# A graph layer's edge messages: three instead of four of a chunk's sixteen node tiles taken by one-hot products, and a whole-array product for the node maxima

## The chip, the cores and the metric

The kernel runs on one core of one Trainium2 chip. The metric is the device time of one execution in microseconds (us); lower is better. A core has five engines with a queue of instructions each: PE (TensorE, matmuls; its weight loads are listed as PEld), DVE (VectorE), ACT (ScalarE), POOL (GpSimd) and SP (SyncE, which here only issues DMAs). They run at the same time and wait for each other by semaphores.

## What is computed

For 400,000 edges (sorted by their target node `dst`) between 12,500 nodes of 32 features:

```
h = relu(layernorm(x))                              # 12500 x 32
e = concat(h[src], h[dst], edge_attr)               # 400000 x 96
v = relu(e @ W1 + b1) @ W2 + b2                     # 96 -> 64 -> 32
out = x + maximum(segment_max(v, dst), h)
```

The costly part is `h[src]`: 400,000 rows of 128 bytes at random places.

## The kernel before

**Tiling.** The edges are cut into 4 stripes of 100,000 (`NS`), and the stripes into 196 chunks (`NCH`) of 512 edges (`C`). A chunk therefore holds 4 x 512 = 2048 edges. Its source rows come as 16 tiles (`K`) of 128 rows: in a tile, partitions 32s to 32s+31 hold 32 edges of stripe s.

**Two ways to a source row.** Of the 16 tiles of every chunk but the last, 12 are gathered and 4 (`MM`) are computed:

- `gather(c)` (L150) has POOL issue one indirect DMA for each gathered tile (L156). Its 128 rows of `h_d` in HBM land in a third of a buffer `gh` that holds `SOME = 3` tiles. There are 24 such buffers; a chunk uses four. POOL issues the gathers of all chunks one after another and stops only where no buffer is free.
- `tile(c, m)` (L229) selects 128 rows of `h` by matmuls. `h` stands in on-chip memory as `hs`, in seven groups of 14 nodes a partition and in two parts whose sum has the full precision. For each of 7 groups and 2 parts a matmul multiplies a one-hot `hot` (128 places x 128 edges) with `hs` (128 places x 448), 14 in all, into a PSUM tile `pv`. DVE multiplies that with a mask (L244) and reduces it (L245) to the 32 features, `gm`. The one-hots of a chunk are made by DVE (`one_hots`, L209, five groups) and ACT (`one_hots_act`, L218 and L219, two groups); their width is `MM` x 128.

`to_features(c, part)` (L247) brings both to a layout with features on partitions: for `part` 0 to 3 DVE transposes one gathered buffer of `SOME` tiles into `ht` (L258), which sets that buffer free for POOL, and for `part = J = 4` it transposes `gm` (L261).

**Main loop** (L535). One turn takes a pair of chunks, and the order of PE, DVE, ACT and SP is written out by hand. With c the pair whose messages are finished and a = c + 2, b = c + 3 the pair whose source rows are being made, PE's order in a turn is: tile(a, 0); the first layer's products with `ht` (L502, `into_ph`); tile(a, 1); tile(a, 2); the first layer's products with the next edge features `ea` (L502); the second layer (L573); the products with the target rows `of` (L502); `leave_2` of chunk c - 1 (L488); tile(a, 3); transposes of chunk c (L478); tile(b, 0); `leave_2` of chunk c; tile(b, 1); transposes of chunk c + 1; tile(b, 2); tile(b, 3). ACT turns the first layer into `hid` (L557); DVE adds a penalty at segment ends and takes a running maximum along the edges in a scan (L580, `sm`), and adds the bias after the transposes (L480, `so`). After each `tile` DVE does that tile's L244 and L245 and the transposes of one gathered buffer.

**PSUM.** `pv` has three buffers. In turn they take each tile's product, the two outputs of the second layer, the transposes and the result of `leave_2`. So a PE step waits for DVE or ACT to have read what stood there three steps before.

**leave_2** (L483) places the maxima of a chunk: for each stripe a window of 32 nodes (`W`), to which `last` holds a one-hot of the last edges. The products are two halves: stripes 0 and 1 into PSUM partitions 0 to 63, stripes 2 and 3 into 64 to 127, four steps of 128 edges each. ACT copies the result to `wo` (L492; three buffers), and SP stores four 32 x 32 blocks to `top_d` (L496), one for each stripe.

Of the kernel before, what the change touches and what calls it, by code (L numbers as in the profile page):

```python
# [8 lines left out]
F32 = mybir.dt.float32  # L9
# [14 lines left out]
P = 128  # L24
N = 12500
E = 400000
D = 32
# [3 lines left out]
NS = 4  # L31
W = 32
C = 512
J = C // P
# [7 lines left out]
LOAD = 4  # L42
A1 = 7
A0 = NT // A1
MM = 4
MMC = range(NCH - 1)
SOME = 3
AHEAD = 4
BLOCK = 14
NB = NCH // BLOCK  # L50
# [12 lines left out]
def ap(t, offset, dims):  # L63
    return bass.AP(tensor=t.tensor, offset=t.offset + offset, ap=dims)
# [3 lines left out]
def gnn_kernel(ctx, tc, x, src, src_mm, src_t, dst, dst_ext, lo, lo_c, ends_b, edge_attr, weights, w1, w2, b2, out):  # L68
# [19 lines left out]
    nc = tc.nc  # L88
# [7 lines left out]
    top_d = [dram.tile([NP, D], F32, name=f"top_d{k}") for k in range(2)]  # L96
    key_d = dram.tile([len(MMC) * MM * P], F16, name="key_d")
    acc_d = dram.tile([NP, D], F32, name="acc_d")
# [31 lines left out]
    hs = const.tile([P, 2, A1, D, A0], F32R, name="hs")  # L130
    place_k = const.tile([P, len(MMC) * MM], F32, name="place_k")

# [17 lines left out]
    def gather(c):  # L150
        n = min(K - MM * (c in MMC), (SE - c * C) // D)
        parts = []
        for k in range(0, n, SOME):
            parts.append(gathered.tile([P, SOME, D], F32, name="gh"))
            for i in range(min(SOME, n - k)):
                nc.gpsimd.indirect_dma_start(  # L156
                    out=parts[-1][:, i, :], out_offset=None, in_=h_d[:, :],
                    in_offset=bass.IndirectOffsetOnAxis(ap=src_i[:, c, k + i:k + i + 1], axis=0))
        return parts
# [3 lines left out]
    early_ps = ctx.enter_context(tc.tile_pool(name="early_ps", bufs=1, space=PSUM))  # L163
# [12 lines left out]
    def group(out, of, last=None):  # L176

        nc.vector.tensor_scalar(out, of, 1.0 / A0, 0.5 / A0 - 0.5, op0=ALU.mult, op1=ALU.add)
        nc.vector.tensor_scalar(out, out, ROUND, None, op0=ALU.add)
        nc.vector.tensor_scalar(out if last is None else last, out, ROUND, None, op0=ALU.subtract)  # L180

    def places(start, stop):

        se = src_i[:, MMC.start + start:MMC.start + stop, K - MM:]
        pk = place_k.rearrange("p (c m) -> p c m", m=MM)[:, start:stop]
        group(pk, se)
        nc.vector.scalar_tensor_tensor(pk, pk, -float(A0), se, op0=ALU.mult, op1=ALU.add)

    def load_keys(c, queue=nc.scalar):

        if c in MMC and c % KEYS == 0:
            n = min(KEYS, MMC.stop - c)
            kb = early.tile([P, KEYS, MM * P], F16, name="kb", bufs=2)
            queue.dma_start(kb[:, :n], ap(key_d, (c - MMC.start) * MM * P,
# [17 lines left out]
    def one_hots_act(c, groups=BY_ACT):  # L212

        if c not in MMC:
            return
        for k in groups:
            away = early.tile([P, MM * P], F32, name="away", bufs=2)
            nc.scalar.activation(away, keys[c], AF.Square, bias=key_n[:, k:k + 1])  # L218
            nc.scalar.activation(hot_of(c)[:, k], away, AF.Relu, bias=ones, scale=-1.0)  # L219

    def mask_of(c):
        if c in MMC:
            masks[c] = early.tile([P, MM, A0], F32, name="mask", bufs=2)
            nc.vector.tensor_tensor(
                masks[c], place_ps[:, None, :].to_broadcast([P, MM, A0]),
                place_k[:, (c - MMC.start) * MM:(c - MMC.start + 1) * MM, None].to_broadcast([P, MM, A0]),
                op=ALU.is_equal)

    def tile(c, m):  # L229

        if c not in MMC:
            return
        if m == 0:
            mm_rows[c] = early.tile([P, MM, D], F32, name="gm", bufs=4)
        hot = hots[c]
        e = slice(m * P, (m + 1) * P)
        po = early_ps.tile([P, C], F32, name="pv", bufs=3)[:, :D * A0]
        for k in range(A1):
            for part in range(2):
                nc.tensor.matmul(po, hot[:, k, e], hs[:, part, k].rearrange("p f a -> p (f a)"),  # L240
                                 start=(k == 0 and part == 0), stop=(k == A1 - 1 and part == 1))
        of_group = po.rearrange("p (f a) -> p f a", a=A0)
        one = early.tile([P, D, A0], F32, name="one", bufs=2)
        nc.vector.tensor_tensor(one, of_group, masks[c][:, m, None, :].to_broadcast([P, D, A0]), op=ALU.mult)  # L244
        nc.vector.tensor_reduce(mm_rows[c][:, m, :], one, axis=AX.X, op=ALU.max)  # L245

    def to_features(c, part):  # L247

        if c >= NCH:
            return  # L250
        if c not in hts:
            hts[c] = early.tile([P, K, D], F32, name="ht", bufs=4)
        ht = hts[c]
        n = min(K - MM * (c in MMC), (SE - c * C) // D)
        if part < J:
            r = slice(part * SOME, min((part + 1) * SOME, n))
            if r.start < n:
                nc.vector.transpose(ht[:, r].rearrange("p k e -> p (k e)"),  # L258
                                    gh[c][part][:, :r.stop - r.start].rearrange("p k f -> p (k f)"))
        elif c in MMC:  # L260
            nc.vector.transpose(ht[:, n:].rearrange("p k e -> p (k e)"),  # L261
                                mm_rows.pop(c).rearrange("p k f -> p (k f)"))
        elif n < K:
            nc.vector.memset(ht[:, n:], 0.0)
# [26 lines left out]
    with tc.tile_pool(name="nodes", bufs=1) as pool, tc.tile_pool(name="nodes_ps", bufs=2, space=PSUM) as ps:  # L291
# [127 lines left out]
        one_hots_act(1, range(3, A1))  # L419
        one_hots(1, 0, 3)  # L420
        mask_of(1)
        for m in range(1, MM):
            tile(0, m)
            to_features(0, m)
        to_features(0, J)
# [3 lines left out]
    with tc.tile_pool(name="edges", bufs=3) as pool, tc.tile_pool(name="edges_ps", bufs=1, space=PSUM) as ps:  # L429
# [52 lines left out]

        def leave_2(c, so, last):  # L483

            pw = early_ps.tile([P, C], F32, name="pv", bufs=3)[:, :2 * D]
            for j in range(J):
                for g in range(2):
                    nc.tensor.matmul(pw[g * 2 * W:(g + 1) * 2 * W],  # L488
                                     last[:, j, 2 * g:2 * g + 2].rearrange("p s w -> p (s w)"),
                                     so[:, j, g * 2 * D:(g + 1) * 2 * D], start=(j == 0), stop=(j == J - 1))  # L490
            wo = pool.tile([P, 2 * D], F32, name="wo")
            nc.scalar.activation(wo, pw, AF.Copy)  # L492
            _, base = windows.pop(c)
            for s in range(NS):
                g = slice(s * W, (s + 1) * W)
                nc.sync.dma_start(top_d[s % 2][bass.ds(base[s], W), :], wo[g, s % 2 * D:(s % 2 + 1) * D])  # L496

        def into_ph(ph, pairs, start, stop):
            for x, (w, e) in enumerate(pairs):
# [18 lines left out]
        for c in range(2):  # L518
            window_hots(c)
        one_hots_act(2)  # L520
        for m in range(MM):
            tile(1, m)
            to_features(1, m)
            if m < 2:
                one_hots(2, *((0, 2), (2, BY_ACT.start))[m])
# [9 lines left out]
        for c in range(0, NCH, 2):  # L535
# [32 lines left out]
            last = [lasts(c)]  # L568
            ph = edges_into(a)
            pv = [early_ps.tile([P, C], F32, name="pv", bufs=3) for x in range(2)]  # L570
# [15 lines left out]
            so = leave_1(c, sms[0])  # L586
# [7 lines left out]
            so = leave_1(c + 1, sms[1])  # L594
# [178 lines left out]
```

## Time and profile before

| | us |
|---|---|
| runs (median; lowest, highest) | 4055.93; 4045.58, 4070.74 |
| the profiled execution | 4066.76 |
| its span, first to last instruction | 4065.0 |
| first gather starts, last gather starts | 23.6, 3936.0 |
| DVE busy, ACT busy | 2232.7, 1106.1 |
| mean granted TensorE clock | 0.939 |

The profile is of one execution. In its group rows stand the line of the kernel, the engine, the operation, what it writes and reads, the number of instructions, then busy us and mean ns of one, then the idle time of that engine just before these instructions and what ended most of it ("issue": nothing that the profile shows). A busy share is an average over the span. The waits that concern the gathers, as the profile adds them up for POOL: it sat idle before a gather 542.8 us until a transpose of a gathered buffer (L258), 455.2 us until the transpose of `gm` (L261), and 619.2 us with nothing shown. A timeline row is a start, a duration and what ran; a window row gives the busy time of each engine in a stretch of the span.

### The profile page before, as it was taken

Reading aid. Unit: us, or ns where it says so; the run is one execution under the profiler, and the core shown is the slowest. Engines: PE = TensorE matmul, PEld = TensorE weight load, DVE = VectorE, ACT = ScalarE, POOL = GpSimd, SP = SyncE. Lnnn points to the kernel's source line nnn. Section 1 sums busy time; section 2 is a strip of 40 time slices with the busy share of each in tenths; the row PEclk is TensorE's granted clock in tenths of the full one; section 3 lists DMA queues with packets and bytes.
Section 4 is the critical chain, followed back from the end, with each engine's and each line's share of the span. In section 5 each row is a group of like instructions: output and inputs, shape, how many; then the busy total and the mean of one; then the engine's idle time right before and its main releaser. Section 6 shows DMA issues by size and latency. Waiting matters only on the chain. (4 is left out here: it accounts for less than half of the span.)

```text
span 4065.0 us, 52812 instructions
## 1 busy us (share of the span) xinstructions
PE 3500.2 (86%) x18053; PEld 2584.2 (64%) x18053; DVE 2232.7 (55%) x3876; ACT 1106.1 (27%) x1795; POOL 2257.0 (56%) x2376
## 2 busy tenths in 40 slices
PE   4688889888888898888988888998888889998896
PEld 3466666666666666666666666666666666666665
DVE  4355556555555555555555555555555555655555
ACT  3122222222222222222222232322222223222231
POOL 6555555555555556555555555555555555555550
PEclk7799999999999999999999999999999999999998
DMA  5122212211222122111322222222122222211221
GB/s 189 46 48 65 52 44 55 68 43 44 54 65 49 44 51 69 46 44 46 71 49 47 62 58 47 44 70 52 44 46 66 53 47 49 70 48 44 57 59 50
DMA packets 188622, 229.27 MB, mean 56 GB/s; under 512 B 117549, under 2 KB 159933, under 8 KB 175550
## 3 DMA queue, kind: packets, MB, share of 16 engines
q10 hardware_dynamic: 26692, 110.63, 8.7%
q1 hardware_dynamic: 86618, 76.67, 7.7%
q0 software_dynamic: 75040, 38.57, 6.3%
q8 instruction: 143, 2.34, 0.2%
q14 instruction: 129, 1.06, 0.1%
HBM read 211.76 MB, written 13.85 MB: 56 GB/s over the span
## 5 line engine op out<-in xcount | busy, mean ns | idle before, releaser
L156 POOL DMA_INDIRECT gh<-h_d,src_i x2345 | 2236.5, 954 | 1685.9 <-issue 619.2
L240 PE MATMUL pv<-hs,hot 128*128 128x448 f32 x10920 | 2434.7, 378 | 231.8 <-issue 166.7
L240 PEld LDWEIGHTS pv<-hs,hot 128*128 128x128 f32 x10920 | 2077.6, 194 | 509.9 <-issue 258.1
L244 DVE TENSOR_TENSOR one<-pv,mask 128x448 f32<-128x448 f32 x780 | 478.3, 613 | 1590.8 <-remote 653.4
L557 ACT ACTIVATE hid<-ph,wt 128x512 f32<-128x512 f32 x392 | 254.6, 686 | 1498.2 <-PE ph L502 920.7
L209 DVE TENSOR_TENSOR hot<-kb,consts 128x1536 fp32r<-128x1536 f16 (+2 forms) x388 | 566.1, 1459 | 0.0
L245 DVE TENSOR_REDUCE gm<-one 128x32 f32<-128x448 f32 x780 | 483.6, 620 | 26.9
L219 ACT ACTIVATE hot<-away,ones 128x512 fp32r<-128x512 f32 x392 | 283.6, 724 | 337.3 <-issue 326.3
L580 DVE TENSOR_TENSOR_SCAN sm<-pb,sm,pv 128x512 f32<-128x512 bf16 x195 | 248.2, 1273 | 150.5 <-remote 114.7
L492 ACT ACTIVATE wo<-pv 128x64 f32<-128x64 f32 x196 | 43.8, 223 | 1052.8 <-PE pv L488 765.0
L573 PE MATMUL pv<-hid,wt 128*64 128x512 f32 x784 | 242.1, 667 | 62.2 <-issue 36.3
L488 PEld LDWEIGHTS pv<-so,last 128*64 128x64 f32 x3136 | 126.0, 140 | 250.7 <-issue 162.0
L488 PE MATMUL pv<-so,last 128*64 128x64 f32 x3136 | 166.1, 232 | 131.9 <-issue 121.7
L218 ACT ACTIVATE away<-kb,key_n 128x512 f32<-128x512 f16 x392 | 277.7, 708 | 0.0
L502 PE MATMUL ph<-ea,wt 64*128 64x512 f32 x784 | 233.8, 632 | 35.2 <-issue 29.8
L502 PE MATMUL ph<-ht,wt 64*128 64x512 f32 x784 | 209.7, 637 | 48.3 <-DVE ht L261 42.7
L258 DVE STREAM_TRANSPOSE ht<-gh 128x96 f32<-128x96 f32 x782 | 209.7, 268 | 0.0
L502 PE MATMUL ph<-of,qw 64*128 64x512 f32 x784 | 206.0, 635 | 2.8 <-issue 2.7
L573 PEld LDWEIGHTS pv<-hid,wt 128*64 128x64 f32 x784 | 57.1, 143 | 235.2 <-issue 161.4
L502 PEld LDWEIGHTS ph<-of,qw 64*128 64x128 f32 x784 | 71.9, 195 | 145.4 <-issue 139.3
L502 PEld LDWEIGHTS ph<-ea,wt 64*128 64x128 f32 x784 | 78.3, 188 | 129.5 <-issue 116.2
L502 PEld LDWEIGHTS ph<-ht,wt 64*128 64x128 f32 x784 | 65.2, 188 | 138.2 <-DVE ht L261 77.8
(78 smaller groups left out, 1014.1 us busy)
## 6 DMA issues: line engine op xcount, KB each, us to landing
ea<-in_edge_attr SPq DMA_DIRECT2D x49, 1024.0 KB
db<-in_dst_ext ACTq DMA_DIRECT2D x48, 1024.0 KB
gh<-h_d,src_i POOLq DMA_INDIRECT x2345
pb<-pen_d ACTq DMA_DIRECT2D x48, 512.0 KB
kb<-key_d ACTq DMA_DIRECT2D x47, 512.0 KB
qw<-q_d SPq DMA_DIRECT2D x784, 8.0 KB
top_d<-wo SPq DMA_DIRECT2D x784, 4.0 KB
top_d<-zero ACTq DMA_DIRECT2D x2, 1568.0 KB
```

The costliest lines, as they stand in the source:

```text
L156: nc.gpsimd.indirect_dma_start(out=parts[-1][:, i, :], out_offset=None, in_=h_d[:, :], in_offset=bass.IndirectOffsetOnAxis(ap=src_i[:, c, ...
L209: nc.vector.tensor_tensor(hot_of(c)[:, start:stop], keys[c][:, None, :].to_broadcast([P, n, MM * P]), key_ps[:, start:stop, None].to_broad ...
L218: nc.scalar.activation(away, keys[c], AF.Square, bias=key_n[:, k:k + 1])
L219: nc.scalar.activation(hot_of(c)[:, k], away, AF.Relu, bias=ones, scale=-1.0)
L240: nc.tensor.matmul(po, hot[:, k, e], hs[:, part, k].rearrange("p f a -> p (f a)"), start=(k == 0 and part == 0), stop=(k == A1 - 1 and par ...
L244: nc.vector.tensor_tensor(one, of_group, masks[c][:, m, None, :].to_broadcast([P, D, A0]), op=ALU.mult)
L245: nc.vector.tensor_reduce(mm_rows[c][:, m, :], one, axis=AX.X, op=ALU.max)
L488: nc.tensor.matmul(pw[g * 2 * W:(g + 1) * 2 * W], last[:, j, 2 * g:2 * g + 2].rearrange("p s w -> p (s w)"), so[:, j, g * 2 * D:(g + 1) * ...
L502: nc.tensor.matmul(ph[2 * x + k], w[g], e[g], start=start, stop=stop)
L557: nc.scalar.activation(hid[s], ph[s], AF.Relu, bias=b1c)
L573: nc.tensor.matmul(pv[x][k * 2 * D:(k + 1) * 2 * D], w2x, hid[2 * x + k], start=True, stop=True)
L580: nc.vector.tensor_tensor_scan(sm, loaded.pop(c + x)[2], pv[x], before, op0=ALU.add, op1=ALU.max)
```

## The change

```diff
-MM = 4
+MM = 3
 MMC = range(NCH - 1)
-SOME = 3
+SOME = 4
...
     def tile(c, m):
 
-        if c not in MMC:
+        if c not in MMC or m >= MM:
             return
...
-        for m in range(1, MM):
+        for m in range(1, J):
             tile(0, m)
             to_features(0, m)
...
         def leave_2(c, so, last):
 
-            pw = early_ps.tile([P, C], F32, name="pv", bufs=3)[:, :2 * D]
+            pw = early_ps.tile([P, C], F32, name="pv", bufs=3)[:, :NS * D]
             for j in range(J):
-                for g in range(2):
-                    nc.tensor.matmul(pw[g * 2 * W:(g + 1) * 2 * W],
-                                     last[:, j, 2 * g:2 * g + 2].rearrange("p s w -> p (s w)"),
-                                     so[:, j, g * 2 * D:(g + 1) * 2 * D], start=(j == 0), stop=(j == J - 1))
-            wo = pool.tile([P, 2 * D], F32, name="wo")
+                nc.tensor.matmul(pw, last[:, j].rearrange("p s w -> p (s w)"), so[:, j],
+                                 start=(j == 0), stop=(j == J - 1))
+            wo = pool.tile([P, NS * D], F32, name="wo", bufs=2)
             nc.scalar.activation(wo, pw, AF.Copy)
...
-                nc.sync.dma_start(top_d[s % 2][bass.ds(base[s], W), :], wo[g, s % 2 * D:(s % 2 + 1) * D])
+                nc.sync.dma_start(top_d[s % 2][bass.ds(base[s], W), :], wo[g, s * D:(s + 1) * D])
...
-        for m in range(MM):
+        for m in range(J):
             tile(1, m)
             to_features(1, m)
```

Three of a chunk's sixteen tiles are computed by one-hot products and 13 are gathered. A gather buffer holds four tiles, so a chunk's gathered rows lie in buffers of 4, 4, 4 and 1, each transposed in one instruction. The calls `tile(a, 3)` and `tile(b, 3)` of the loop do nothing; the transposes behind them stay, of the buffer with one tile. `leave_2` multiplies all 128 window rows with all 128 columns of `so` in one matmul for each step of 128 edges, and the four 32 x 32 blocks on the diagonal are what is stored; its two copies `wo` are twice as wide, and there are two instead of three.

## The prediction

> **What bounds the kernel now.** I read the page first, then the waits, then timelines and windows of single stretches.
>
> ```profile
> PE 3500.2 (86%) x18053; PEld 2584.2 (64%) x18053; DVE 2232.7 (55%) x3876; ACT 1106.1 (27%) x1795; POOL 2257.0 (56%) x2376
> ...
> L156 POOL DMA_INDIRECT gh<-h_d,src_i x2345 | 2236.5, 954 | 1685.9 <-issue 619.2
> ```
>
> Taken alone this says that TensorE is the bound. The pairs of chunks say otherwise. Below, columns are the window, its length, then busy time and instructions of PE, PEld, DVE, ACT, POOL, the granted clock, the DMA share and GB/s.
>
> ```profile
> 56.00:137.00 81.00, 17.59 (x36) 9.71 (x36) 7.21 (x22) 5.45 (x8) 61.05 (x64) 0.52 0.35 105
> ...
> 3954.90:3987.60 32.70, 32.70 (x186) 25.17 (x184) 22.29 (x38) 10.88 (x18) 0.44 (x1) 1.00 0.02 5
> 2001.00:2039.00 38.00, 36.54 (x185) 25.99 (x185) 21.97 (x38) 11.20 (x18) 22.91 (x25) 0.96 0.41 96
> ```
>
> The last two rows hold the same work, one pair. After the last gather (3936.0 us) a pair takes 32.7 us with TensorE without a hole; with gathers beside it this one takes 38.0, and the mean from the first scan (172 us) to the one at 3920 is 39.9. The first row is the extreme: POOL issues 64 gathers without a pause, and TensorE gets 36 records done in 81 us, where a matmul of a tile normally follows the last after 0.21 us. So a long unbroken run of gathers holds up the other engines. In the steady part it shows as signals that come late (timeline of DVE, then of POOL; columns: start, duration, what, the idle time before it and what ended that):
>
> ```profile
> 2021.65 0.27 DVE L258 STREAM_TRANSPOSE ht<-gh 128x96 f32<-128x96 f32 x1
> 2021.84 1.18 DVE L209 TENSOR_TENSOR hot<-kb,consts 128x1024 fp32r<-128x1024 f16 x1
> 2032.56 0.62 DVE L244 TENSOR_TENSOR one<-pv,mask 128x448 f32<-128x448 f32 x1 [9.53 <-PE ph L502]
> ```
>
> ```profile
> 2015.46 0.95 POOL L156 DMA_INDIRECT gh<-h_d,src_i  x1 [1.56 <-DVE ht L258]
> 2016.71 0.95 POOL L156 DMA_INDIRECT gh<-h_d,src_i  x1 [0.30 <-issue]
> ...
> 2029.48 0.95 POOL L156 DMA_INDIRECT gh<-h_d,src_i  x1 [0.44 <-issue]
> 2034.29 0.95 POOL L156 DMA_INDIRECT gh<-h_d,src_i  x1 [3.86 <-DVE ht L258]
> ```
>
> The product that DVE waits for ended at 2025.2 in TensorE's records. DVE starts 7.3 us later, 2.1 us after POOL's run ended at 2030.4. POOL stopped because all 24 gather buffers were full, and it goes on once that same DVE step has emptied one. Over the steady part I grouped the gathers into runs (a new run where two starts lie over 1.45 us apart): 125 runs of 6, 33 of 9, 60 of 12, 15 of 15, with mean gaps behind them of 2.6, 2.7, 3.4 and 10.2 us. A product that ends 7 to 11 us into a run is typically seen 5 to 7 us late, about 2 us after the run's end. In runs of 15 TensorE works at full rate until 13 us after the run's start and at 2 to 6% of it from 15 to 21 us. So POOL's time is the sum to count: a gather takes 0.952 + 0.305 us (median duration, plus the idle that always follows), 1.257 us, and the span is 23.6 (first gather) + 2345 x 1.257 = 2947.7 + gaps + 127.8 (from the end of the last, 3936.0 + 1.257, to 4065.0), which leaves 966 for the gaps. The group's row agrees: 1685.9 less 2345 x 0.305 is 971. Per pair that is 9.9 us of gaps beside 24 x 1.257 = 30.2 of gathers.
>
> **The change, part by part.** *Gathers.* 195 chunks gather 13 tiles for 12: 195 more, 2540 x 1.257 = 3192.8, so +245.1 on POOL. Nothing hides it where POOL never pauses but for full buffers.
>
> *Products removed.* Two tiles less per pair, each 14 matmuls in 2.9 us on TensorE and 0.613 + 0.620 us on DVE. One-hots narrow from 1024 and 1536 columns (1.18 and 1.73 us) to 768 and 1152; by their slope 0.90 and 1.32, 1.4 us less DVE per pair. A gathered transpose of 96 or 128 columns takes 0.268 or 0.269 alike: zero. ACT's narrower one-hots, and the product's copy, twice as wide (0.223 us, bounded by the 0.69 of a 512-wide op), lie under ACT's idle 1052.8 before that copy.
>
> *Whole-array product (leave_2).* Sixteen 64-column records now take 0.61 us from group to group; eight of 128 columns are bounded by 0.61 (same columns, half the instructions) and 1.22 (all of the present overlap lost). In the rows four 512-column pairs take 1.92 us, 0.43 per 512; 1024 columns one after another give 0.86. I take 0.9: +0.6 us per pair. The Trainium skill (TensorEngine Tiling (Array Packing), Performance Considerations) says that 64-column operands pack two tiles side by side, so this step should cost up to twice; by it alone the sum would take 1.22, another +0.6 us per pair of TensorE work, and 59 us over 98 pairs if TensorE were the bound.
>
> *Output buffers three to two.* A copy waits for the stores of two chunks ago; they are issued 30 us earlier (stores at 2008.98 to 2017.2, the second copy after at 2046.7) and land in microseconds: nothing. Were that cover gone, ACT would hold up a PSUM buffer and, behind it, the next one-hots.
>
> So a pair has 32.7 - 5.8 + 0.6 = 27.5 us of TensorE work, and needs 26 x 1.257 = 32.7 us of POOL. The last three pairs, without gathers, gain 5.2 each: the tail is 127.8 - 15.6 = 112.2.
>
> *Gaps.* This is the unknown. Between their bounds I sketch one pair, with 0 where DVE has emptied tile 1 of the first chunk. POOL starts at 0.5. DVE does one-hots 1.3, a mask 0.2, tile 2 (1.24 + 0.27): empty at 3.0. Then 0.65 and two scans (2.6): at 6.3 the last scan gives back the PSUM buffer that tile 0 of the second chunk needs, and the 1-gather buffer follows at 6.6. (TensorE waits for these scans: tile 3 stood in front of the transposes L478 and covered 2.9 us of it. Queued behind L478 is that tile 0.) POOL has spent 4 + 4 + 1 = 9 gathers by 11.8. Tile 0 ends at 6.3 + 2.9 = 9.2, 8.7 us into the run, so its signal comes 2 us after the run, at 13.8; empty at 15.4, POOL on at 15.9: a gap of 4.1. Second run: 4, then 4 (17.9), 4 and 1 (22), 4 (24): 17 gathers, 21.4 us, to 37.3. The next tile's product ends at about 27, deep in the run; signal 39.3, empty 40.9, gap 4.1 again. Period 40.9, gaps 8.2. The same sketch for the kernel before gives 38.5 with gaps of 8.3, where 9.9 are measured (ratio 1.19). So the freed TensorE time does not shorten the gaps: they come from the late signals. Low end: if a product signalled in the run comes through (it does where TensorE had just waited, lag 0.04 us), the second run is 21 long and the gaps are 4.2 + 1.6 = 5.8. High end: the 10.2 us behind the runs of 15, say 10.5 per pair. I take 8.7, between the sketch and the sketch times 1.19 (9.8): over 98 pairs 853.
>
> Sum: 23.6 + 3192.8 + 853 + 112.2 = 4182 for the profiled execution's span, +117 on 4065. That execution took 4066.8, 10.8 above the median of 4055.9; less that, 4170.
>
> **The rivals.** *TensorE is the bound after all* (86% busy, late signals only harmless). Then the gathers hide in POOL's 44% of idle time until POOL itself binds: 23.6 + 3192.8 + 112.2 + 2 us of gap per pair (196) = 3525, less 11: 3514. For it: the records; against it: the 36 records in 81 us. The Trainium skill (SBUF — State Buffer, Who interferes with whom) says that DMA never contends with a compute engine, only GpSimd and VectorE share a port; by that the gathers would not slow TensorE and this rival's 3514 would come. The trace disagrees: 38.0 against 32.7 us for equal work. *One long run per pair*: gaps of 5.8, 568 in all, 3897 less 11: 3886. For it: TensorE will wait at the ht products (one tile of cover instead of two), and after such waits signals came through. *Break-even*: gaps of 7.5, 735 in all, cancel the 245; 4053. *Collapse*: two buffers of 4 emptied behind each other make runs beyond 13 us common, each with a gap like 10.2; 11 per pair, 1078 in all: 4396. For it: tiles of 4 instead of 3, so runs are 4/3 as long for as many emptied buffers; against it: the 1-gather buffer breaks them. It decides once the mean run passes some 13 gathers. That the edit isn't what it says is no rival: in the changed program's order a chunk has three 14-matmul tiles and its fourth transposes gathered data alone.
>
> **How the numbers follow.** My forecast, gaps of 8 to 10 per pair (4102 to 4298): 0.48. TensorE bound 0.10, one long run 0.18, break-even 0.12, collapse 0.12. The range leaves out the first rival and most of the collapse: 3885 to 4350; the likeliest case's own is 4100 to 4300. This kernel's runs spread over 0.6%, so 1% is what can be told. Faster 0.28 (first two rivals), same 0.12, slower 0.60.
>
> **What would show it.** Gathers: 2540 of 0.95 us with 0.305 behind each. The group's idle: about 775 + 853. Runs of 8 to 17 in place of 6 to 12, and DVE's product of the first chunk's tile 1 again some 2 us after a run's end. A pair without gathers near 27.5 us, with gathers near 41. PE's share should fall to about 70%. I am wrong if gaps per pair fall under 7, or if a gather's pitch moves.

## The result, and the profile after

The changed kernel takes 4097.9 us (median of 8 runs, 4086.7 to 4119.4) and the kernel before 4057.9 beside it (8 runs, 4036.1 to 4070.7): a ratio of 1.0108, 95% interval 1.0079 to 1.0137. It is slower by some 1%; the forecast was 4170 us, 2.8% above 4056. The profiled execution took 4102.3 us, its span is 4099.9.

The page of the changed kernel, the line of busy times and two groups:

```profile
PE 3283.4 (80%) x13755; PEld 2178.5 (53%) x13755; DVE 1863.2 (45%) x3486; ACT 1037.4 (25%) x1795; POOL 2440.5 (60%) x2571
...
L156 POOL DMA_INDIRECT gh<-h_d,src_i x2540 | 2420.0, 953 | 1555.5 <-DVE ht L258 763.8
...
L487 PE MATMUL pv<-so,last 128*128 128x128 f32 x1568 | 229.3, 291 | 86.8 <-DVE so L480 82.4
```

TensorE has 217 us less of busy time than before and the kernel is longer. POOL has the 2540 gathers at the old 0.953 us. Of its idle time, 763.8 us ended with a transpose by VectorE (L258) that emptied a gather buffer: POOL stands with all buffers full, some two times a pair. Its span adds up as before: 23.3 us to the first gather, 2540 x 1.257 = 3192.8, gaps of 774.0 (summed over the starts of the gathers), and 109.8 behind the last one. That is 7.9 us of gaps a pair, where the kernel before had 9.9.

One turn of the pattern, in windows of the changed kernel (columns as in the prediction: window, length, busy time and instructions of PE, PEld, DVE, ACT, POOL, clock, DMA share, GB/s). It begins with a run of 17 gathers (2021.8), which ends at 2043.1; POOL then stands until 2047.6 and makes a run of 9:

```profile
2021.80:2034.80 13.00, 13.00 (x66) 10.70 (x65) 7.82 (x16) 2.33 (x4) 9.95 (x11) 1.00 0.65 143
2034.80:2043.20 8.40, 4.10 (x12) 1.33 (x10) 0.00 (x0) 5.33 (x9) 6.19 (x7) 0.93 0.38 113
2043.20:2047.60 4.40, 2.91 (x8) 1.34 (x9) 1.74 (x4) 0.00 (x0) 0.00 (x1) 0.50 0.26 95
2047.60:2058.90 11.30, 10.69 (x57) 7.50 (x55) 6.92 (x12) 2.52 (x5) 8.57 (x9) 0.94 0.09 15
```

For 13 us TensorE starts 5 matmuls a us beside the gathers, then 1.4 a us until the run ends, and VectorE starts nothing at all. VectorE's timeline over the same time (start, duration, what, idle time before it and what ended that), and TensorE's:

```profile
2029.41 0.92 DVE L209 TENSOR_TENSOR hot<-kb,consts 128x768 fp32r<-128x768 f16 x1
2045.83 0.63 DVE L244 TENSOR_TENSOR one<-pv,mask 128x448 f32<-128x448 f32 x1 [15.50 <-PE ph L500]
2046.49 0.62 DVE L245 TENSOR_REDUCE gm<-one 128x32 f32<-128x448 f32 x1
2047.03 0.30 DVE L258 STREAM_TRANSPOSE ht<-gh 128x128 f32<-128x128 f32 x1
```

```profile
2029.80 5.88 PE L240 MATMUL pv<-hs,hot 128*128 128x448 f32 x28
2035.61 1.13 PE L500 MATMUL ph<-ea,wt 64*128 64x512 f32 x4
2037.32 0.59 PE L500 MATMUL ph<-ea,wt 64*128 64x512 f32 x1 [0.58 <-issue]
2039.43 0.59 PE L500 MATMUL ph<-ea,wt 64*128 64x512 f32 x1 [1.52 <-issue]
2042.22 1.01 PE L500 MATMUL ph<-ea,wt 64*128 64x512 f32 x1 [2.20 <-issue]
```

TensorE's two tiles are done at 2035.7 at the latest. The product that waits for the first of them starts at 2045.8, 2.7 us after the gathers stop; its transpose at 2047.0 empties the buffer on which POOL goes on at 2047.6. "Issue" on TensorE's lines is time in which it waited for nothing that the profile knows.

Two more windows of the changed kernel: the first lies in its first long run of gathers, the second behind its last gather (what POOL does there is another instruction, L545):

```profile
56.00:137.00 81.00, 22.38 (x32) 9.16 (x32) 7.07 (x23) 5.01 (x8) 61.20 (x66) 0.50 0.32 93
...
4001.00:4028.00 27.00, 27.00 (x142) 20.68 (x140) 18.18 (x34) 10.14 (x18) 9.51 (x1) 1.00 0.10 32
```

At the end, with no gathers, a pair takes 27.5 us from scan to scan and TensorE has no hole. At the start, beside 66 gathers in one run, TensorE gets 32 records done in 81 us.

How late a signal is can be counted over the whole trace, from the end of the last of a tile's 14 matmuls to the start of the product on VectorE that waits for it (L244, waits of over 1 us, from 200 us on). In this run 197 of 233 such products start over 2 us late, with a median of 4.0 us; in the kernel before it is 183 of 351, with a median of 2.0.

### The profile page after: what moved, and what is told of

It is laid out like the page before. It is cut to its first block, busy times and chain, and to the rows that moved or that the text cites. A ratio compares the mean times of both kernels' runs of the same rounds, so it can differ in the third digit from the quotient of the medians.

```text
span 4099.9 us, 44559 instructions
## 1 busy us (share of the span) xinstructions
PE 3283.4 (80%) x13755; PEld 2178.5 (53%) x13755; DVE 1863.2 (45%) x3486; ACT 1037.4 (25%) x1795; POOL 2440.5 (60%) x2571
## 3 DMA queue, kind: packets, MB, share of 16 engines
q0 software_dynamic: 81280, 41.78, 6.5%
## 5 line engine op out<-in xcount | busy, mean ns | idle before, releaser
L156 POOL DMA_INDIRECT gh<-h_d,src_i x2540 | 2420.0, 953 | 1555.5 <-DVE ht L258 763.8
L240 PE MATMUL pv<-hs,hot 128*128 128x448 f32 x8190 | 1821.4, 374 | 174.7 <-issue 155.2
L240 PEld LDWEIGHTS pv<-hs,hot 128*128 128x128 f32 x8190 | 1532.4, 192 | 395.3 <-issue 256.8
L244 DVE TENSOR_TENSOR one<-pv,mask 128x448 f32<-128x448 f32 x585 | 360.6, 616 | 1879.8 <-remote 1300.7
L500 PE MATMUL ph<-ea,wt 64*128 64x512 f32 x784 | 444.3, 795 | 297.0 <-issue 261.2
L209 DVE TENSOR_TENSOR hot<-kb,consts 128x1152 fp32r<-128x1152 f16 (+2 forms) x388 | 436.2, 1124 | 0.0
L487 PE MATMUL pv<-so,last 128*128 128x128 f32 x1568 | 229.3, 291 | 86.8 <-DVE so L480 82.4
L487 PEld LDWEIGHTS pv<-so,last 128*128 128x128 f32 x1568 | 200.7, 197 | 184.3 <-issue 116.1
L219 ACT ACTIVATE hot<-away,ones 128x384 fp32r<-128x384 f32 x392 | 241.3, 616 | 18.5 <-issue 5.7
L218 ACT ACTIVATE away<-kb,key_n 128x384 f32<-128x384 f16 x392 | 235.7, 601 | 0.0
L258 DVE STREAM_TRANSPOSE ht<-gh 128x128 f32<-128x128 f32 (+1 forms) x782 | 205.4, 271 | 0.0
```

The costliest lines, as they stand in the source:

```text
L156: nc.gpsimd.indirect_dma_start(out=parts[-1][:, i, :], out_offset=None, in_=h_d[:, :], in_offset=bass.IndirectOffsetOnAxis(ap=src_i[:, c, ...
L209: nc.vector.tensor_tensor(hot_of(c)[:, start:stop], keys[c][:, None, :].to_broadcast([P, n, MM * P]), key_ps[:, start:stop, None].to_broad ...
L487: nc.tensor.matmul(pw, last[:, j].rearrange("p s w -> p (s w)"), so[:, j], start=(j == 0), stop=(j == J - 1))
L500: nc.tensor.matmul(ph[2 * x + k], w[g], e[g], start=start, stop=stop)
```

## The experiments

Two theories were put on record: G, that POOL's gathers and the gaps that late signals make bound the kernel, and T, that TensorE does. Within G, G1 says that making and moving gathers holds the others up, and G2 that any busy POOL does. In the first two batches below, and in the comparison above, the kernel before took 4036 to 4058 us. In the three later batches the same kernel, from the same source, took 3298 to 3299 us. Ratios are always against the kernel before of the same batch, on the same chip. The only trace of the kernel before is that of the comparison above.

### First batch (before: 4036.1 us)

**The whole-array leave_2 alone**, in the kernel before (four tiles, parts of three gathers):

```diff
-                for g in range(2):
-                    nc.tensor.matmul(pw[g * 2 * W:(g + 1) * 2 * W],
-                                     last[:, j, 2 * g:2 * g + 2].rearrange("p s w -> p (s w)"),
-                                     so[:, j, g * 2 * D:(g + 1) * 2 * D], start=(j == 0), stop=(j == J - 1))
+                nc.tensor.matmul(pw, last[:, j].rearrange("p s w -> p (s w)"), so[:, j],
+                                 start=(j == 0), stop=(j == J - 1))
-            wo = pool.tile([P, 2 * D], F32, name="wo")
+            wo = pool.tile([P, NS * D], F32, name="wo", bufs=2)
```

> The kernel before with the whole-array leave_2 alone (four products a chunk, wo in two buffers; still four tiles a chunk by matmuls). Theory G (POOL's gathers and the gaps that late signals make bound the kernel): 2345 gathers as before, gaps of about 966 us as before, so 4058 us within 1%, because the 0.6 us a pair that TensorE loses or gains is not what the pair waits for. Rival T (TensorE bounds): the whole-array group took 0.81 to 0.99 us against 0.61 us in the traces, two a pair, so +0.4 to +0.8 us a pair, +39 to +74 us, a time of 4097 to 4132 us, and the whole of the change's +1% would be here.

4119.3 us, 1.0216 (1.0178 to 1.0253). G missed. T's range in us holds this time only because the kernel before was 22 us faster in this batch: T wanted 39 to 74 us more than before, and 83 came. The gaps are 1020 us, 54 more than the 966 in the trace of the kernel before, and the two spans (4121.2 and 4065.0) differ by 56: what was added is POOL standing still.

**The tiles alone**: MM = 3 and SOME = 4 with the split leave_2 and three wo buffers.

> The change without its whole-array leave_2: three tiles a chunk by matmuls, thirteen by gathers, the split leave_2 and three wo buffers of before. Theory G: 2540 gathers at 1.257 us and gaps as in the changed kernel (774 us), so 4098 us within 1%: the whole of the slowdown is here. Rival T: 39 to 74 us faster than the changed kernel, 4024 to 4059 us.

4325.5 us, 1.0737 (1.0708 to 1.0765). Both missed, T by more: with less of TensorE's work than the kernel before, it is 7% slower. The gaps are 989 us, 10.1 a pair. So the parts alone cost 2.2% and 7.4%, and together 1.1%: their sizes don't add, and the whole-array product (with its two `wo` buffers), dear alone, takes 215 us of gaps (989 less 774) out of the kernel with three tiles.

**Half of the product matmuls** in the changed kernel:

```diff
-            for part in range(2):
-                nc.tensor.matmul(po, hot[:, k, e], hs[:, part, k].rearrange("p f a -> p (f a)"),
-                                 start=(k == 0 and part == 0), stop=(k == A1 - 1 and part == 1))
+            nc.tensor.matmul(po, hot[:, k, e], hs[:, 0, k].rearrange("p f a -> p (f a)"),
+                             start=(k == 0), stop=(k == A1 - 1))
```

> The changed kernel with half of the tile products: the matmuls with the low part of hs are left out (the output lacks that part), 7 matmuls of 128x392 fewer for each of 6 tiles a pair, some 8.7 us of TensorE's 27.5 us a pair. Theory G: gathers stay at 2540 x 1.257 = 3193 us; the gaps shrink by what the late signals carried of this work, at most from 7.9 to about 4 us a pair, so 3720 to 4100 us; I take 3950 us. Rival T (TensorE bounds): 98 x 8.7 = 853 us less, 3250 us or a little more.

4041.8 us, 1.0021 (0.9992 to 1.0051): by the ratios 0.9% of before, some 35 us, less than the changed kernel, where T wants 853. TensorE's busy time fell from 3283 to 2515 us for it. (The matmuls left out have 448 columns, not 392 as the expectation says.) G's range held; its 3950 was too low, for the gaps shrank only from 774 to 727 us.

**Twelve gathers for thirteen** in the changed kernel:

```diff
-        for k in range(0, n, SOME):
+        for k in range(0, min(n, J * (SOME - 1)), SOME):
...
-                                    gh[c][part][:, :r.stop - r.start].rearrange("p k f -> p (k f)"))
+                                    gh[c][min(part, 2)][:, :r.stop - r.start].rearrange("p k f -> p (k f)"))
```

> The changed kernel with twelve instead of thirteen gathers for each of the first 195 chunks (the thirteenth tile is the transpose of the first row block of the third part once more, so the output is of the wrong nodes there); TensorE, VectorE and ScalarE do what they did. Theory G: 195 x 1.257 = 245 us less of gathers, with gaps between 7 and 11 us a pair as in the other patterns, so 3780 to 4150 us; I take 3853 us, gaps unchanged. Rival T: no change, 4098 us within 1%.

3927.0 us, 0.9735 (0.9713 to 0.9757), by the ratios 3.7%, some 150 us, less than the changed kernel. No other engine's work was taken away, so T is out here. (A chunk now holds three buffers and not four, so the 24 buffers reach two chunks further; what that does was not run alone.) Between the two profiled spans (4099.9 and 3922.6) lie 177 us: of the 245 us of gathers, 35 came back as gaps (809) and 32 as a longer tail (142).

### Second batch (before: 4039.9 us)

**No gathers after the first six chunks**; later chunks transpose those rows again:

```diff
         parts = []
+        if c >= 6:
+            return gh[c - 6]
```

> The changed kernel without the gathers of chunks 6 to 195 (those chunks transpose the rows gathered for chunks 0 to 5 again, so their messages are of the wrong nodes); TensorE, VectorE and ScalarE do what they did. Theory G (POOL's stream and the lateness that it causes in the others): the pairs without gathers at the end of the changed kernel's trace took 27.5 us, so some 150 + 97 x 27.5 + 110 = 2930 us, at most 3100 us where the granted clock falls. Rival T (TensorE bounds): no change, 4098 us within 1%.

2853.2 us, 0.7062 (0.7003 to 0.7121). The 97 pairs take 27.5 us each as forecast; around them are 184 us and not the 260 of the forecast, so its 2930 us was too high. A window of it:

```profile
2000.00:2027.00 27.00, 27.00 (x142) 20.52 (x140) 18.37 (x34) 10.14 (x18) 0.00 (x0) 1.00 0.35 89
```

It is the window 4001 to 4028 of the changed kernel once more, in the middle of the program. The 12.9 us between 27.5 and the 40.4 of a usual pair are due to the gathers. And no signal is late: all 284 products that VectorE waited for start 0.04 us after their last matmul.

**Memsets in the gathers' place**:

```diff
+                if c >= 6:
+                    nc.gpsimd.memset(parts[-1][:, i, :], 0.0)
+                    nc.gpsimd.memset(pause, 0.0)
+                    continue
```

> The changed kernel with each gather of chunks 6 to 195 replaced by two POOL memsets, one of the same 128x32 tile and one of a 128x1024 scratch tile, about 1.2 us together, so that POOL is as long busy and the waits for the buffers are the same, but no descriptors are made and no rows move (the messages of those chunks are of zeros). Theory G1 (what holds the others up is the making and moving of gathers): the others run freely beside POOL, the period goes to POOL's own 26 x 1.2 to 1.3 us and a small wait, 33 to 36 us a pair, 3300 to 3650 us. Rival G2 (any busy POOL holds them up): as the changed kernel, 3950 to 4150 us. Rival T: 4098 us within 1%.

3273.1 us, 0.8102 (0.8034 to 0.8170). Two rows of its groups, and windows:

```profile
L159 POOL MEMSET pause<- 128x1024 f32 x2462 | 2345.8, 953 | 110.5
L158 POOL MEMSET gh<- 128x32 f32 x2462 | 190.5, 125 | 447.1 <-DVE ht L263 443.5 <-issue 3.5
```

```profile
56.00:137.00 81.00, 23.64 (x48) 11.53 (x47) 7.07 (x23) 5.43 (x9) 58.25 (x77) 0.55 0.37 104
2000.00:2032.00 32.00, 30.26 (x140) 22.15 (x140) 17.63 (x32) 10.15 (x18) 30.56 (x54) 0.91 0.11 24
600.00:2600.00 2000.00, 1779.57 (x8198) 1299.12 (x8199) 1124.17 (x2052) 595.70 (x1056) 1912.90 (x3461) 0.90 0.20 50
2700.00:3050.00 350.00, 349.35 (x1781) 264.01 (x1778) 239.04 (x447) 126.66 (x226) 25.64 (x330) 1.00 0.24 62
```

The order on POOL is not that of the source. Of the kernel's engines POOL alone has no order written out by hand, and the long memsets, which wait for no buffer, run ahead of their places: some 33 a pair beside 26 short ones, until the last at 2685.5 us. So this is not POOL at the gathers' pitch, and the 3273 us is a mixture: up to there a pair takes 34.1 us, and behind it 27.5.

It decides between G1 and G2 all the same. At the start, where it still gathers, TensorE starves as ever (48 matmuls in 81 us). From 600 to 2600 us POOL is busy for 96% of the time, against 60% in the changed kernel with its pairs of 40.4 us, and the pair of 34.1 is little more than POOL's own 32.6 us of work. TensorE makes 140 matmuls in 32 us there, and all 266 products that VectorE waited for start 0.04 us after their last matmul. A busy POOL makes no signal late; gathers do: G1. Whether it is the making of a gather or the moving of its rows was not run apart.

**Pauses between gathers**, a memset after every four, or after each:

```diff
             for i in range(min(SOME, n - k)):
                 nc.gpsimd.indirect_dma_start(
...
+            if n - k >= SOME:
+                nc.gpsimd.memset(pause, 0.0)
```

> The changed kernel with a POOL memset of a 128x512 scratch tile, about 0.55 us, after every four gathers: six a pair, 3.3 us of POOL. Theory G with a backlog that a short break drains: the gaps of 7.9 us a pair shrink by more than 3.3 us, 36 to 39 us a pair, 3650 to 3950 us. Theory G with a backlog that needs a wait of some 2 us to drain, so that short breaks are only added to POOL's stream: 40.5 + 1 to 3.3 us a pair, 4150 to 4420 us. Rival T: no change, 4098 us within 1%.

> The changed kernel with a POOL memset of a 128x128 scratch tile, about 0.2 us, after every gather: 26 a pair, 5.2 us of POOL or, if it fits into the 0.3 us between two gathers, nothing. Theory G with a rate limit (what the others get done beside gathers grows with the gathers' spacing): the gaps shrink by more than what is added, 36 to 40 us a pair, 3650 to 4050 us. Theory G with a backlog that only an end of the stream drains: 4150 to 4600 us. Rival T: no change.

4368.6 us, 1.0814 (1.0722 to 1.0905), and 4626.1 us, 1.1451 (1.1336 to 1.1565). Neither tests what it was made for, because here too the memsets ran ahead of their places. From the second kernel, POOL's timeline:

```profile
711.93 0.95 POOL L157 DMA_INDIRECT gh<-h_d,src_i  x1 [0.30 <-issue]
712.88 3.11 POOL L160 MEMSET pause<- 128x128 f32 x12
716.49 0.96 POOL L157 DMA_INDIRECT gh<-h_d,src_i  x1 [0.49 <-issue]
717.45 10.01 POOL L160 MEMSET pause<- 128x128 f32 x38
```

The pauses come in bunches. The last one is at 1001 us in the first kernel and at 1731 us in the second. While they last a pair takes 52.8 and 57.9 us (medians), of which some 20 are pauses. So what a short break inside a run of gathers does stays open.

What is left behind the last pause tells something else. There both kernels issue just what the changed kernel does, and yet the gaps are 9.0 us a pair (1200 to 4200 us, and 1900 to 4400 us), where the changed kernel has 8.0 from 300 to 3900 us. The same instructions settle into different patterns of stops, worth 1 us a pair.

### Third and fourth batch (before: 3297.7 and 3297.6 us)

These were made to find what in leave_2 moves the gaps: its number of products (two column halves, eight products), the wo buffers (three), or its place (leave() ahead of tile(a, 2)).

```diff
+            for g in range(2):
+                r = slice(g * 2 * D, (g + 1) * 2 * D)
+                for j in range(J):
+                    nc.tensor.matmul(pw[:, r], last[:, j].rearrange("p s w -> p (s w)"), so[:, j, r],
+                                     start=(j == 0), stop=(j == J - 1))
-            for j in range(J):
-                nc.tensor.matmul(pw, last[:, j].rearrange("p s w -> p (s w)"), so[:, j],
-                                 start=(j == 0), stop=(j == J - 1))
```

```diff
-            wo = pool.tile([P, NS * D], F32, name="wo", bufs=2)
+            wo = pool.tile([P, NS * D], F32, name="wo")
```

```diff
             mask_of(b)
+            leave()
             tile(a, 2)
...
             windows_into(a, ph)
-            leave()
```

> The changed kernel with leave_2's whole-array product cut into two column halves, eight products of 64 columns a chunk instead of four of 128, one PSUM tile, one copy and two wo buffers as in the change. Theory N (in the stretch of a gather run in which TensorE issues under one matmul a us, the number of its instructions counts, not their length; the split leave_2 has 4 more there before the products whose signals end POOL's two stops): the stops lengthen as in tiles_alone, 4325 us within 2%. Rival W (it is the wo buffers, or the copy of 128 columns, that make tiles_alone slower than the change): 4098 us within 1%. Rival R (it is the rhythm into which the pairs fall, that any small shift moves): anything between 4050 and 4350 us, with other lengths of runs than 9 and 17.

> The changed kernel with three wo buffers instead of two, all else as it is. Theory N: nothing waits for the two buffers, 4098 us within 1%. Rival W (the buffers matter): outside of that, towards tiles_alone's 4325 us if three are worse.

> The changed kernel with the call leave() (leave_2 of the pair before: four matmuls, a copy and four DMAs) moved from behind windows_into to ahead of tile(a, 2). Theory N: four matmuls leave the long stretch of TensorE's order between the second chunk's first tile and the tile before it, so POOL's stop ahead of the second chunk's first part (3.4 us a pair in the changed kernel) falls by about 1.5 us, and the one at the first chunk's second part stays: 3950 us, between 3900 and 4060. Theory R: the rhythm breaks, 4100 to 4350 us. Rival T (TensorE bounds): no change, 4098 us.

> As memsets (each gather of chunks 6 to 195 replaced by a memset of the same tile and one of a scratch tile, so no descriptors and no rows), with a scratch tile of 1275 columns instead of 1024, so that two memsets take about 1.257 us as a gather does. Theory G1 (making and moving of gathers holds up the others; a busy POOL does not): POOL's stream becomes 26 x 1.257 = 32.7 us a pair, its waits shrink from the 4.6 us of memsets to 1 to 3 us, 3350 to 3600 us. Rival G2 (a busy POOL, at its gathers' own pitch, holds up the others): 3950 to 4150 us.

3287.9, 3286.8 and 3281.6 us, ratios 0.9972, 0.9971 and 0.9958, all intervals within 0.9944 to 0.9982. The memsets with the wider scratch tile took 3330.7 us, 1.0104, under the 3350 forecast: a pair mostly takes 33.7 to 33.9 us with POOL busy for 97% of 600 to 2600 us. They ran ahead of their places too, until 3199 us, and made no signal late. None of the numbers on record came. The kernel before itself was 740 us faster, and gathers held up nothing. The first three were run again with the changed kernel itself beside them:

> The changed kernel itself, beside the three that follow. The last four kernels ran on a chip on which the kernel before took 3298 us, and POOL's gathers went on without stops. If the chip is of that kind: POOL's stream bounds, 23.3 + 2540 x 1.257 + 98 x 0.24 + some 50 of tail, 3285 us within 0.5%, 0.996 of before. If it is of the kind on which before takes some 4040 us: 1.011 of before within 0.7%.

> The changed kernel with leave_2's product in two column halves (eight products instead of four). On a chip on which the gathers hold up the others: theory N (the number of TensorE's instructions in the starved stretch) about as tiles_alone, 1.05 to 1.08 of before; rival W (wo buffers, copy) 1.01; rival R (rhythm) anything from 1.0 to 1.08 with other run lengths than 9 and 17. On a chip on which they don't: 0.997 of before.

> The changed kernel with three wo buffers instead of two. On a chip on which the gathers hold up the others: theory N 1.01 of before within 1%; rival W towards 1.07; rival R anything between. On a chip on which they don't: 0.997 of before.

> The changed kernel with leave() moved ahead of tile(a, 2). On a chip on which the gathers hold up the others: theory N 3950 us, 0.965 to 1.0 of before, POOL's stop ahead of the second chunk's first part about 1.5 us shorter than 3.4; rival R 1.01 to 1.08 with the rhythm broken. On a chip on which they don't: 0.996 of before.

The changed kernel took 3281.8 us, 0.9955 (0.9939 to 0.9972), as expected for a chip where gathers hold up nothing; the others 0.9965, 0.9958 and 0.9957, no different from it. A third run of the eight products, in the last batch, gave 0.9968 (0.9958 to 0.9978):

> The changed kernel with leave_2's product in two column halves (eight products instead of four), once more, for a chip on which the gathers hold up the others. There: theory N (the number of TensorE's instructions in the starved stretch) about as tiles_alone, 1.05 to 1.08 of before; rival W (wo buffers, copy) 1.01; rival R (rhythm) anything from 1.0 to 1.08 with other run lengths than 9 and 17. On a chip on which they don't: 0.9965 of before, as twice before.

What these batches do tell is in the page of the changed kernel run again, beside which stand the same lines of the result above:

```profile
PE 2873.5 (88%) x13755; PEld 2120.1 (65%) x13755; DVE 1892.3 (58%) x3486; ACT 1020.0 (31%) x1795; POOL 2441.5 (74%) x2571
...
L156 POOL DMA_INDIRECT gh<-h_d,src_i x2540 | 2421.2, 953 | 803.0 <-issue 572.4
...
L244 DVE TENSOR_TENSOR one<-pv,mask 128x448 f32<-128x448 f32 x585 | 359.6, 615 | 429.4 <-PE pv L240 428.7
```

and in its first 81 us of gathers:

```profile
56.00:137.00 81.00, 63.89 (x288) 44.59 (x286) 38.21 (x71) 25.02 (x43) 61.50 (x65) 0.85 0.42 120
```

It is the same program, with the same gathers at the same 1.257 us, 65 of them in this window as against 66. TensorE made 32 records beside them there and 288 here. POOL's idle time of 803.0 us is little but the 0.305 us behind each gather (2540 x 0.305 = 775); the gaps are 22.7 us in all, and all but 34 of the gathers lie in runs of 45 to 208. All 199 products that VectorE waited for start 0.04 us after their last matmul. The whole is 23.7 + 3192.8 + 22.7 + 39.1 = 3278.3: POOL's stream with nothing in it to shorten but gathers. How many matmuls TensorE starts per us, by the time since a run of gathers began (worked out from the two traces, for runs between 300 and 3900 us; runs split at starts more than 1.45 us apart):

```
us into the run     0-4   4-8   8-12  12-16  16-20  20-30  30-60
in the result      3.57  4.82   4.88   2.80   0.58   0.53      -
run again          4.34  4.62   5.04   5.35   5.48   4.77   3.84
```

The gathers' own rows are no slower where the others are held up. In the run of the result the packets of the gathers' queue (q0) take 6.5% of 16 engines' span, in the run again 9.4%, for the same 81280 packets: 52 and 61 ns each. The last of a gather's packets starts a median of 2.03 us after the gather in the first, and 2.13 us in the second. A rival, that row packets pile up in the DMA engines late in a run, finds no support in these two traces.

### Last batch (before: 3299.3 us)

**A version between the two**: four tiles by matmuls in even chunks, three in odd ones, the split leave_2, gather parts of four in 18 buffers.

```diff
+    def mm(c):
+        return (MM - c % 2) * (c in MMC)
...
-        n = min(K - MM * (c in MMC), (SE - c * C) // D)
+        n = min(K - mm(c), (SE - c * C) // D)
...
-        e = slice(m * P, (m + 1) * P)
+        km = m + MM - mm(c)
+        e = slice(km * P, (km + 1) * P)
```

> A version between the two: four tiles by matmuls in the even chunks, three in the odd ones, the split leave_2 of before, gather parts of four in 18 buffers instead of 24 (for space), key and mask code still for four tiles. 2443 gathers, TensorE's work per pair 32.7 - 2.9 = 29.8 us. On a chip on which the gathers hold up nothing: POOL's stream bounds, 23.3 + 2443 x 1.257 = 3094 us, + 98 x 0.24 of gaps + some 50 of tail = 3168 us, 0.96 of before, faster than the change (0.9955). Rival on such a chip: 18 buffers are too few, and TensorE's and POOL's waits add up, 1.0 of before. On a chip on which they hold up the others: 3094 + 98 x (8 to 10) + 115 = 3993 to 4190 us, 0.99 to 1.04 of before. Rival T (TensorE bounds on every chip): 98 x 2.9 = 284 us less than before, 0.93.

3172.0 us, 0.9612 (0.9596 to 0.9628), faster than the kernel before and, by the ratios, than the changed kernel (0.9955 in the batch before); forecast 3168 for this case. Its busy times, and the head of its gathers' view:

```profile
PE 3005.4 (95%) x16695; PEld 2245.7 (71%) x16695; DVE 2135.4 (67%) x3584; ACT 1091.5 (34%) x1795; POOL 2350.4 (74%) x2473
```

```profile
L159 POOL DMA_INDIRECT gh<-h_d,src_i x2442: 946/952/2210, 23.7 to 3128.8; - x188
...
  issue: 549.2, 1760
```

23.7 + 2442 x 1.257 = 3069.6, + 36.8 of gaps + 44.9 = 3175.0, its span. POOL still bounds, with TensorE at 95% close behind. Where gathers hold the others up this version wasn't run.

## Why the prediction was right and wrong

**The bound: right for the runs compared, and not a law of gathers.** That POOL's stream and the gaps in it set the time, not TensorE's 86%, is shown by four runs: 7.8 us a pair less of busy TensorE gave some 0.4 us (half_product); 195 gathers less gave 150 to 177 us (twelve_gathers); no gathers gave 27.5 us a pair; memsets that keep POOL busier gave 34.1 us a pair, with no late signal. But the sentence "So a long unbroken run of gathers holds up the other engines" holds in some runs and not in others. The Trainium skill (SBUF — State Buffer, Who interferes with whom) says, of the ports of the on-chip memory, that DMA never contends with a compute engine. The batches at 3298 us agree with it (288 records in 81 us); in those at 4036 to 4058 us gathers do hold TensorE up (32), and no run shows whether those ports are the place. In the batches at 3298 us the rival "TensorE is the bound after all" is true of the kernel before: 98 pairs of the 32.7 us that a pair without gathers took are 3205 of 3298 us, though no trace of it was taken there. The change then moves the bound from TensorE to POOL's 26 x 1.257 = 32.7 us a pair, and the time stays (0.9955). The rival's 3514 us for it was too high, by 2 us of gap a pair (0.2 measured) and by a tail of 112 us (39). What sets the one or the other isn't known. It isn't simply the chip: the chip of the first two batches and that of the last carry the same number, and the kernel before took 4036 us on it first and 3299 later.

**Gathers**: 2540 at 0.952 + 0.305 us, +245 us on POOL, as forecast, nothing hiding it.

**Products removed**: a pair without gathers takes 27.5 us, the number forecast. That this would not shorten the time is what half_product shows.

**leave_2**: the group of matmuls took 0.81 and 0.99 us at the two places, around the 0.9 taken, and under the estimate of 1.22 that follows from the Trainium skill's rule (TensorEngine Tiling (Array Packing), Performance Considerations). But in the sum the product enters only through the tail. What it does to POOL's stops had no term, and there the prediction saw nothing of what came: +2.2% alone, and 6% less in the kernel with three tiles (1.0108 for 1.0737).

**wo buffers**: three instead of two give the same time where the gathers hold up nothing (3284 and 3287 for 3282 us); where they do it wasn't measured.

**Gaps: the step that failed.** The pattern is the one sketched: 77 runs of 9 and 71 of 17 gathers between 300 and 3900 us, and 77 of some 95 pairs with 26 gathers in 40.5 us (sketch: 40.9). The mean stop behind a run of 9 is 3.29 us and that behind 17 is 4.55 (sketch: 4.1 each). The prediction then put on top of it: "I take 8.7, between the sketch and the sketch times 1.19 (9.8): over 98 pairs 853." Measured are 774, 7.9 a pair, nearer to the 7.5 at which the change would have broken even. These 79 us are nearly all of the 82 between the 4182 forecast for the span and 4099.9; the tail gave 2 (109.8 for 112.2). The bare sketch, 8.2 x 98 = 804, would have given 4133. The factor 1.19 came from the kernel before, where the sketch's one pattern is rare: of its pairs 37 have 24 gathers, in 39.4 us, 21 have 27 in 42.8 and 19 have 21 in 40.0. So, as far as these counts show, it measured how far that kernel strays from a steady pattern, and was laid on one that keeps to it; that is argued from the counts, and no run tests it. (The prediction's mean pair of that kernel, 39.9 us, is itself a miscount: from the scan at 172 us to that at 3920 are 93 pairs, 40.3 each.)

That the bare sketch comes near is in part luck. No step of it depends on how `leave_2` is done, and for the three tiles alone, with 10.1 a pair, it would have been 1.9 us a pair too low, and the factor 1.19 nearly right.

The rivals within G did not come. Of one long run a pair, with 21 gathers behind the 9, the pattern shows nothing: its longer runs are of 17. The collapse priced long runs by the 10.2 us behind the runs of 15 in the kernel before; the runs of 17 here cost 4.55 us each. (In those runs of 15 TensorE's rate from 15 to 21 us is some 0.75 starts a us against 4 to 5, about a sixth, and not the 2 to 6% that the prediction reads.)

Where POOL stops, from the traces (mean over 85 pairs, us a pair; a and b are the pair's chunks, the number the gather before which it stops):

```
before          a3 2.56  a6 0.25  a9 4.75   b3 1.47  b6 0.99             10.1
whole_alone     a3 1.53  a6 1.24  a9 5.28   b3 0.72  b6 2.02             10.9
tiles_alone     a0 1.96  a4 0.87  a8 0.25   a12 1.17  b0 5.00 b4 0.21 b8 0.84   10.3
after           a0 0.25  a4 3.93  a12 0.20  b0 3.41                       8.0
```

Stops of under 0.2 us a pair are left out of the rows, and counted in the sums. In these four kernels, two main stops a pair at fixed places cost less than more stops that wander. Why the whole-array leave_2 brings the kernel with three tiles into the fixed pattern stays open: the number of products, the wo buffers and the place of the step were each run, but in batches where there was no hold-up to see. That the same instructions gave 9.0 us a pair behind the pauses says that the instructions alone do not settle the pattern.

**Marks named ahead.** POOL's group was idle for 1555.5 us (forecast 1628), runs were of 9 and 17, and the product of the first chunk's tile 1 came 2.7 us after the run's end (forecast some 2). A pair with gathers takes 40.4 us (forecast near 41). TensorE's share is 80%, not 70%. Its records stretch where it starves: the same 13755 matmuls count 3283 us here, at a mean granted clock of 0.866, and 2873 in the run without hold-up, at 0.945. So a part of the 3500 before was probably not work either.

## What to carry to other kernels

When two engines lose time to each other, find a stretch in the trace where one is absent, and price the change against both; an engine's busy share may hold its starvation. A pattern that was sketched from the order of waits is better left as it is than scaled by another pattern's error. Read the order of instructions in an experiment's own trace before its time: four kernels here were written to put memsets between or in place of gathers, and the memsets ran elsewhere. And run the kernel before beside every experiment: here the base moved by 740 us, and a change that costs 1% in one condition gains 0.5% in the other, where a balance between the two kernels gains 4%.

## What the runs showed of the hardware

- The same kernel took 4036 to 4058 us in some batches and 3298 to 3299 in others, steadily within each (4021 to 4050 in 13 runs, 3293 to 3303 in 20). In the former, in the changed kernel, TensorE starts 0.5 to 0.6 matmuls a us once a run of gathers is 16 us old, in the latter 3.8 to 5.5. What sets the condition is open. The granted clock alone is not it: it is 1.00 in the window 2021.8 to 2034.8 at full rate and 0.93 in the starved one behind it, and where it falls to 0.50 (56 to 137 us) that is a factor of two, where the records are 32 for 288.
- Where gathers hold the others up, they also make signals late: VectorE starts a median of 4.0 us after the last matmul that it waits for. In the run without hold-up, and in the runs without gathers, it starts after 0.04 us.
- A busy POOL alone does this to nobody: 30.6 us of memsets in 32 us left TensorE at 140 matmuls, and the signals at 0.04 us.
- In both conditions a gather holds POOL for the same 0.952 + 0.305 us, and its row packets take 52 and 61 ns.
- In this kernel a signal that was late came 2.1 and 2.7 us after the run of gathers ended, in the two timelines shown. Breaks shorter than that were not tested.
